# Four graph layers on one core: x turned by vector blocks and by DRAM instead of TensorE, short reciprocals, and products that fit either TensorE tile mode

## The chip, the cores and the metric

The kernel runs on one core of a Trainium2 chip. The metric is device time in microseconds (us), the median of several executions. Beside it stands one execution taken by the hardware profiler; all spans and durations come from that one. The engines are PE (TensorE, matrix products; PEld is its weight load), DVE (VectorE), ACT (ScalarE), POOL (GpSimd) and SP (SyncE, which only issues transfers). A record of PE is one pass: a float32 product makes two records, a transpose makes one.

## The reference

32 independent graphs of 512 nodes, each node with 256 features, go through four layers. Each layer ends in a residual sum and a layernorm. All of it is float32.

```python
# layer 0: h = (1+eps) x + adj @ x ;  x = LN(x + relu(h W1 + b1) W2 + b2)
# layer 1: graph attention, 4 heads: softmax over j of leaky_relu(e_dst_i + e_src_j) where adj > 0.5
#          x = LN(x + attention @ (x W) + bias)
# layer 2: 8 heads of 32: softmax over j of (q_i . k_j / sqrt(32) + log(adj + 1e-6))
#          x = LN(x + concat(heads) Wo.T + bo)
# layer 3: softmax over j of ((x W)_i . x_j * adj_ij), masked by nodemask ;  x = LN(x + attention @ x)
```

Products with x as the inner operand need x with features on the partitions (x transposed: 256 features in two tiles of 128 by 512 nodes). After each layernorm x has nodes on the partitions, so layers 1, 2 and 3 each begin by turning x.

## The kernel before, in words

`fast_path` first prepares the weights (`prepare`) and then handles the graphs one by one (`graph(g)`, 32 times). Nothing is emitted directly: each piece of work is a *step* of a `Plan`, with its engine, an assumed cost in us, the steps it comes after, and the buffers it takes and frees. `Plan.order` then walks through time with these costs and writes one order for all engines, a few graphs overlapping; which step goes first is set by a due time from the period and a long list of offsets by step name (the argument of `plan.run`). `Plan.run` emits the steps in that order. Each engine, and each DMA queue of SP and POOL, handles its instructions strictly in it; between engines there are semaphores. So a step that is late holds up everything behind it on its engine.

A PE step has a *mode*: the shape in which the 128x128 array is used. `""` is the whole array, `row` four tiles of 32 rows (layer 2's scores, L1203), `c32` four tiles of 32 columns (attention times values, L1043 and L1261; sums, L1081 and L1330), `r64` tiles of 64 rows and 32 columns (layer 2's sums, L1308). The planner adds the cost `CHANGE` of the new mode when it changes.

The steps around the change, by name and line, for one graph:

- `h`, `f`, `y` (L812, L835, L854): layer 0's three products, whole array. `residual_steps`, `norm_stats` and `norm_steps` (L681, L624, L641, L647, L655, L670) follow every layer: DVE adds to x and gathers statistics, POOL takes the power for rstd, DVE makes the shift, ACT scales x (`r`).
- `xt1`/`xe1`, layer 1's turn of x: 8 PE transposes into PSUM (L882) and two ACT copies. `v1` (L903): values.
- `features_first(2)` and `features_first(3)`, the turns of x for layers 2 and 3: 8 PE transposes (L1147) and two ACT copies (L1151) each. Then `q`, `k`, `v2` (L1166, L1184) for layer 2, and `i`, `t` (L1412, L1427) for layer 3; `p` (L1385) is layer 2's output product, `w` (L1456) is layer 3's attention times x.
- `normalise(o)`: layer 2's softmax denominators arrive in PSUM as [128, 512], where the 32 partitions of a head hold the same numbers. ACT copies them to SBUF (L1344), DVE takes the reciprocal of all 512 columns in two halves (`rc`, L1351), and multiplies y with it (`yd`, L1356).
- `la`: from the second graph on, adj is loaded in four transfers that read runs of 32 numbers (128 bytes), so that the 32x32 blocks lie turned round; four DVE transposes, which turn each 32x32 block in place, then finish the transpose (`at`, L778).
- `collect`, `fd`: POOL issues transfers that add layer 2's weights onto each other in SBUF, so that fewer sums are left to PE.

Of the kernel before, what the change touches and what calls it, by code (L numbers as in the profile page):

```python
# [9 lines left out]
F32 = mybir.dt.float32  # L10
# [38 lines left out]
class Plan:  # L49
# [12 lines left out]

    CHANGE = {"": 0.207, "row": 0.218, "c32": 0.143, "c64": 0.161, "r64": 0.166}
# [69 lines left out]
    def order(self, period, ahead, window, stay, rush=(), moves=(), edges=(0, (), 0, ())):  # L133
# [35 lines left out]
        while low < len(self.steps):  # L169
            found = []  # L170
            for (g, name), t in ready.items():
                s = self.steps[g][name]
                t = max(t, engine.get(s.eng, 0.0))
                change = self.CHANGE[s.mode] if s.eng == "pe" and s.mode != mode else 0.0
                for k, (kind, _, rest) in enumerate(s.take):
                    r, n = room[kind], sum(b[0] == kind for b in s.take[:k])
                    if len(r) <= rest + n:
                        break
                    t = max(t, r[n][0])
                else:  # L180
                    due = turn[g] * period - self.left[g][name] + shift(g, name) + stay * change
                    found.append((t, due, g, name, change))
            if not found:
                return math.inf, out
            first = min(found)[0] + near(low)
            _, t, g, name, change = min((due, t, *f) for t, due, *f in found if t <= first)
            s = self.steps[g][name]
            t += change
            if s.eng == "pe":
                mode = s.mode  # L190
            del ready[g, name]
            got = {}
            for kind, key, _ in s.take:
                got[key] = held[g][key] = (kind, room[kind].pop(0)[1])
            if s.eng:
                engine[s.eng] = t + s.us
            end = ends[g][name] = t + s.us
            last = max(last, end)
            out.append((g, name, t, got))
            for h, n in s.then:  # L200
                waits[h][n] -= 1
                if not waits[h][n] and h < opened:
                    ready[h, n] = self.ready(h, n, ends)
            for k in s.frees:
                fwaits[g][k] -= 1
                if not fwaits[g][k]:
                    key, after = self.frees[g][k]
                    kind, i = held[g].pop(key)
                    free = max(ends[g][a] + self.HOP.get(self.steps[g][a].eng, 0.0) for a in after)
                    room[kind].append((free, i))  # L210
                    room[kind].sort()
            todo[g] -= 1
            while low < len(self.steps) and not todo[low]:
                low += 1
                open_to(low + window)
        return last, out

    def run(self, tries):

        self.link()  # L220
        best = min((self.order(*t)[0], t) for t in tries)
        assert best[0] < math.inf
        for g, name, _, got in self.order(*best[1])[1]:
            self.slot[g].update((key, i) for key, (_, i) in got.items())
            self.steps[g][name].emit()
# [3 lines left out]
def fast_path(  # L229
# [103 lines left out]


# [249 lines left out]
    def graph(g):  # L584
        plan.graph()
        slot = plan.slot[-1]
        last = g == B - 1
        t = {"g": g}
# [101 lines left out]

        if g == 0:
# [73 lines left out]
        else:  # L765
# [16 lines left out]
            @step("atd", "dve", 0.6, row("at", NC))  # L782
            def _():
                full = t["AT"][:, 0, :]
                nc.vector.tensor_add(
                    t["ATd"],
                    bass.AP(full.tensor, full.offset, [list(full.ap[0]), [N + P, NC], [1, P]]),
                    selfw[:, None, :].to_broadcast([P, NC, P]),
                )
# [3 lines left out]
        for d in range(DC):  # L793

            @step(
                f"h{d}", "pe", 3.49,
                (("atd",) if g else row("ate", NC) + row("atd", NC)) + prev("h", d) + ("lx",),
                take=(f"p=h{d}",) + (() if d else ("C=hT",)),
            )
            def _(d=d):  # L800
                if d == 0:
                    t["hT"] = mid("hT", [P, DC, N], "hT")
                ph = t[f"ph{d}"] = bank(f"h{d}", [P, N], f"hT_ps_{d}")
                parts = []
                for m in range(NC):
                    parts.append((m, t["ATd"][:, m, :], blk(m)))
                    if m > 0:
                        parts.append((m, t["AT"][:, m, : m * P], slice(0, m * P)))
                    if m < NC - 1:
                        parts.append((m, t["AT"][:, m, (m + 1) * P :], slice((m + 1) * P, N)))  # L810
                for k, (m, moving, cols) in enumerate(parts):
                    nc.tensor.matmul(  # L812
                        ph[:, cols], t["x"][:, m, blk(d)], moving,
                        start=(k == 0), stop=(k == len(parts) - 1),
                    )
# [8 lines left out]
        for f in range(HC):  # L824
# [3 lines left out]
                take=(f"p=f{f}",) + (() if f else ("B=h1T/2",)),  # L828
            )
            def _(f=f):  # L830
# [3 lines left out]
                for d in range(DC):  # L834
                    nc.tensor.matmul(  # L835
                        ph, w1_sb[:, d, blk(f)], t["hT"][:, d, :], start=(d == 0), stop=(d == DC - 1)
                    )
# [9 lines left out]
        for c2 in range(NC // 2):  # L847

            @step(f"y{c2}", "pe", 3.45, row("fe", HC) + prev("y", c2) + ("^w2",), take=(f"p=y{c2}",))
            def _(c2=c2):  # L850
                py = t[f"py{c2}"] = bank(f"y{c2}", [P, 2, D], f"y0_ps_{c2}")
                for j in range(2):
                    for f in range(HC):
                        nc.tensor.matmul(  # L854
                            py[:, j, :], t["h1T"][:, f, blk(2 * c2 + j)], w2_sb[:, f, :],
                            start=(f == 0), stop=(f == HC - 1),
# [35 lines left out]
        for c in range(NC):  # L892
# [3 lines left out]
                take=(f"p=v1{c}",) + (() if c else ("C=v1",)),  # L896
            )
            def _(c=c):
# [3 lines left out]
                for d in range(DC):  # L902
                    nc.tensor.matmul(  # L903
                        pv, t["xT"][:, d, blk(c)], wg_sb[:, d, :], start=(d == 0), stop=(d == DC - 1)
                    )
# [247 lines left out]
        features_first(2, ("L2",))  # L1153
        bias_steps(3, row("xt2", DC))

        def proj(n, o):
            @step(
                f"{n}{o}", "pe", 1.72, row("xe2", DC) + prev(n, o) + (f"^we{n}",),
                take=(f"p={n}{o}",) + (() if o else (f"C={n}",)),
            )  # L1160
            def _():
# [3 lines left out]
                for d in range(DC):  # L1165
                    nc.tensor.matmul(  # L1166
                        pq, wT[n][:, d, blk(o)], t["xT2"][:, d, :], start=(d == 0), stop=(d == DC - 1)
                    )
# [5 lines left out]
        def values(c):  # L1174
            @step(
                f"v2{c}", "pe", 0.86, row("xe2", DC) + prev("v2", c) + ("^wev",),
                take=(f"p=v2{c}",) + (() if c else ("C=v2",)),
            )
            def _():
# [3 lines left out]
                for d in range(DC):  # L1183
                    nc.tensor.matmul(  # L1184
                        pv, t["xT2"][:, d, blk(c)], wT["v"][:, d, :], start=(d == 0), stop=(d == DC - 1)
                    )
# [153 lines left out]
        def normalise(o, after):  # L1340
            @step(f"nd{o}", "act", 0.49, (after,), take=(f"D=rdT{o}/1",), free=(f"d2{o}",))
            def _():
                t[f"rd{o}"] = strip(f"rdT{o}", [P, N], f"rdT_{o}")
                nc.scalar.copy(t[f"rd{o}"], t[f"d{o}"])  # L1344

            for i in range(2):
                half = slice(i * N // 2, (i + 1) * N // 2)

                @step(f"rc{o}{i}", "dve", 1.65, (f"nd{o}",))
                def _(half=half):  # L1350
                    nc.vector.reciprocal(t[f"rd{o}"][:, half], t[f"rd{o}"][:, half])  # L1351

                @step(f"yd{o}{i}", "dve", 0.34, (f"rc{o}{i}", f"no{o}"))
# [24 lines left out]
        for c2 in range(NC // 2):  # L1378

            @step(f"p{c2}", "pe", 1.73, (f"yd0{c2}", f"yd1{c2}") + prev("p", c2) + ("^weo",), take=(f"p=p{c2}",))  # L1380
            def _(c2=c2):
                py = t[f"py{c2}"] = bank(f"p{c2}", [P, 2, D], f"o2p_ps_{c2}")
                for j in range(2):
                    for d in range(DC):
                        nc.tensor.matmul(  # L1385
                            py[:, j, :], t["yT2"][:, d, blk(2 * c2 + j)], wT["o"][:, d, :],
                            start=(d == 0), stop=(d == DC - 1),
# [12 lines left out]
        features_first(3, ("L3",), src="x3")  # L1400
        for o in range(DC):
# [3 lines left out]
                take=(f"p=i{o}",) + (() if o else ("C=iT",)),  # L1405
            )
            def _(o=o):
# [3 lines left out]
                for d in range(DC):  # L1411
                    nc.tensor.matmul(  # L1412
                        pq, w3_sb[:, d, blk(o)], t["xT3"][:, d, :], start=(d == 0), stop=(d == DC - 1)
                    )
# [6 lines left out]
        for c in range(NC):  # L1421

            @step(f"t{c}", "pe", 1.72, row("ie", DC) + prev("t", c), take=(f"p=t{c}",))
            def _(c=c):
                pt = t[f"pt{c}"] = bank(f"t{c}", [P, N], f"s3_{c}")
                for d in range(DC):
                    nc.tensor.matmul(  # L1427
                        pt, t["xT3"][:, d, blk(c)], t["iT"][:, d, :],
                        start=(d == 0), stop=(d == DC - 1),
                    )  # L1430
# [19 lines left out]
        for c in range(NC):  # L1450

            @step(f"w{c}", "pe", 1.74, row("te", NC) + ("one",) + prev("w", c), take=(f"p=w{c}",))
            def _(c=c):
                py = t[f"py{c}"] = bank(f"w{c}", [P, D + 1], f"o3_ps_{c}")
                for m in range(NC):
                    nc.tensor.matmul(  # L1456
                        py, t[f"z3{m}"][:, blk(c)], t["x3"][:, m, :],
                        start=(m == 0), stop=(m == NC - 1),
                    )
# [538 lines left out]
```

## Time and profile before

| | before |
|---|---|
| median of 3 runs | 2814.2 us (2812.86 to 2814.27) |
| profiled execution, its own time | 2813.72 us |
| its span, first to last instruction | 2812.0 us |
| PE busy | 2777.1 us, 99% |
| DVE busy | 2235.4 us, 79% |
| ACT busy | 1774.5 us, 63% |
| software DMA queue (POOL's), share of 16 engines | 51.2% |
| hardware DMA queue (SP's) | 17.3% |
| granted TensorE clock | 0.997 |

A row of the cost groups reads: line, engine, operation, output and inputs by the program's names, shapes, count; then busy time in all and the mean of one in ns; then the idle time of the engine just before, and what ended it. A row of the timeline reads: start, length, engine, line, operation, names, shapes, count of instructions merged into the row, and in brackets the idle time before with what ended it. In the view by stretches a line gives the length, then for PE, PEld, DVE, ACT and POOL the busy time and the count, the clock and the DMA engines' share and rate. For PE the shape of the stationary tile comes first (128*32: 128 rows by 32 columns), then what streams through it. PE's records overlap, so its prices are read from start to start.

### The profile page before, as it was taken

What the parts mean: (1) busy time and instruction counts of PE and PEld (TensorE: products, weight loads), DVE (VectorE), ACT (ScalarE), POOL (GpSimd) and SP (SyncE); (2) the same over time, 40 slices, a digit from 0 to 9 for tenths busy, and PEclk for the clock granted to TensorE, in tenths of its full rate; (3) what the DMA queues carried; (4) which work ended last, traced back from release to release, by engine and by line L of the source; (5) the groups of instructions that cost most, each with busy time, mean ns of one, the idle gap of its engine ahead of it and who ended that gap; (6) DMA issues with size and microseconds to landing.
All of it is one profiled execution on the core that took longest, in us unless ns stands there. A gap on an engine that the chain in (4) does not pass through costs nothing.

```text
span 2812.0 us, 41564 instructions
## 1 busy us (share of the span) xinstructions
PE 2777.1 (99%) x15540; PEld 1549.1 (55%) x15540; DVE 2235.4 (79%) x4139; ACT 1774.5 (63%) x3438; POOL 450.9 (16%) x526
## 2 busy tenths in 40 slices
PE   8999999999999999999999999999999999999998
PEld 6544565555555555555555655555555555555544
DVE  3878779877779877788877788777798777887785
ACT  3767566676666675666665666766666756666564
POOL 1111111111111111111111111111111111111110
PEclk9999999999999999999999999999999999999999
DMA  8476777667787667786677776667776677667650
GB/s 172 90 160 123 154 143 155 134 137 145 145 158 145 131 139 146 139 171 134 137 141 148 143 160 133 135 143 149 153 144 135 139 146 143 136 134 137 135 104 16
DMA packets 350055, 388.74 MB, mean 138 GB/s; under 512 B 265036, under 2 KB 304920, under 8 KB 317976
## 3 DMA queue, kind: packets, MB, share of 16 engines
q0 software_dynamic: 45568, 277.89, 51.2%
q1 hardware_dynamic: 303296, 107.86, 17.3%
q8 instruction: 124, 2.03, 0.3%
q14 instruction: 83, 0.68, 0.1%
q10 hardware_dynamic: 984, 0.28, 0.0%
HBM read 141.38 MB, written 17.08 MB: 56 GB/s over the span
## 4 chain that ended last, share of the span: by engine, by line
PE 92%; DVE 3%; DMA 2%; ACT 2%; issue 1%; POOL 0%; ACTq 0%; SPq 0%; DVEq 0%; POOLq 0%
PE s L1203 9%; PE hT_ps L812 8%; PE o_ps L1261 8%; PE o_ps L1043 8%; PE h1T_ps L835 8%; PE s L1427 8%; PE o_ps L1456 7%; PE y_ps L854 7%; PE v_ps L903 4%; PE iT_ps L1412 4%; PE qT_ps L1166 4%; PE v_ps L1184 4%; PE o2p_ps L1385 4%; PE kT_ps L1166 4%; PE xT_t L1147 2%; DMA z<-z 1%
## 5 line engine op out<-in xcount | busy, mean ns | idle before, releaser
L1216 ACT ACTIVATE z<-s 128x512 f32<-128x512 f32 x1024 | 535.5, 605 | 214.4 <-PE s L1203 208.1
L1225 DVE SCALAR_TENSOR_TENSOR z<-AT,z 128x1024 f32<-128x1024 f32 x512 | 601.3, 1213 | 13.0 <-ACT z L1216 12.6
L1236 POOL DMA_DIRECT2D z<-z x186 | 164.1, 889 | 1686.2 <-DVE z L1225 522.8
L1351 DVE RECIPROCAL rdT<-rdT 128x256 f32<-128x256 f32 x128 | 214.3, 1721 | 229.2 <-ACT rdT L1344 229.2
L1010 ACT ACTIVATE z<-R_bc,nT,S 128x512 f32<-128x512 f32 x512 | 372.6, 814 | 3.3 <-DMA R_bc<-R_dram 3.2
L1021 DVE SCALAR_TENSOR_TENSOR z<-z,T,edge 128x512 f32<-128x512 f32 x512 | 347.4, 745 | 16.4 <-ACT z L1010 16.2
L670 ACT ACTIVATE x<-x,shift,rstd 128x256 f32<-128x256 f32 x508 | 264.0, 591 | 75.9 <-DVE shift L655 74.6
L1203 PE MATMUL s<-qT,kT 32*128 32x512 f32 x2048 | 288.9, 633 | 0.4 <-ACT kT L1172 0.4
L1261 PE MATMUL o_ps<-z,v 128*32 128x512 f32 x2048 | 264.2, 600 | 3.1 <-DVE z L1225 2.1
L1456 PE MATMUL o_ps<-x,z 128*128 128x257 f32 x1024 | 240.3, 386 | 3.2 <-ACT z L1216 2.5
L1071 DVE TENSOR_TENSOR z<-z 128x1024 f32<-128x1024 f32 (+1 forms) x256 | 237.0, 951 | 4.2 <-PE o_ps L1043 2.7
L1043 PE MATMUL o_ps<-z,v 128*32 128x512 f32 x2048 | 237.2, 599 | 0.0
L835 PE MATMUL h1T_ps<-hT,w_sb 128*128 128x512 f32 x512 | 234.3, 599 | 0.0
L1456 PEld LDWEIGHTS o_ps<-x,z 128*128 128x128 f32 x1024 | 189.2, 189 | 77.9 <-issue 46.3
L1427 PE MATMUL s<-iT,xT 128*128 128x512 f32 x512 | 229.3, 599 | 0.0
L854 PE MATMUL y_ps<-w_sb,h1T 128*128 128x256 f32 x1024 | 226.6, 379 | 0.0
L624 DVE BATCH_NORM_STATS2 st<-x 128x6 f32<-128x256 f32 x508 | 211.5, 416 | 9.3
L812 PE MATMUL hT_ps<-AT,x 128*128 128x384 f32 (+2 forms) x768 | 210.7, 384 | 0.5 <-ACT AT L761 0.5
L854 PEld LDWEIGHTS y_ps<-w_sb,h1T 128*128 128x128 f32 x1024 | 194.0, 190 | 27.4 <-ACT z L1216 0.8
L647 POOL TENSOR_TENSOR rstd<-ve,nhalf 128x4 f32<-128x4 f32 (+1 forms) x131 | 141.1, 1077 | 356.8 <-DVE ve L641 347.7
L841 ACT ACTIVATE h1T<-h1T_ps,b_sb 128x512 f32<-128x512 f32 x128 | 87.9, 687 | 147.7 <-PE h1T_ps L835 147.7
L1203 PEld LDWEIGHTS s<-qT,kT 32*128 32x128 f32 x2048 | 88.7, 183 | 160.8 <-issue 74.1
(162 smaller groups left out, 3763.2 us busy)
## 6 DMA issues: line engine op xcount, KB each, us to landing
z<-z POOLq DMA_DIRECT2D x186, 1024.0 KB, 8.2
x<-biases POOLq DMA_DIRECT2D x96, 512.0 KB, 9.6
R_bc<-R_dram SPq DMA_DIRECT2D x32, 1024.0 KB, 4.6
Ar<-in_adj_dram SPq DMA_DIRECT2D x124, 256.0 KB, 7.5
z<-z POOLq DMA_DIRECT2D x62, 512.0 KB, 7.0
x<-in_x_dram SPq DMA_DIRECT2D x32, 512.0 KB, 9.0
out_dram<-x SPq DMA_DIRECT2D x31, 512.0 KB, 4.1
xs_row<-xs_dram SPq DMA_DIRECT2D x32, 128.0 KB, 5.6
```

The lines of the kernel that those rows point to most:

```text
L812: nc.tensor.matmul(ph[:, cols], t["x"][:, m, blk(d)], moving, start=(k == 0), stop=(k == len(parts) - 1),)
L835: nc.tensor.matmul(ph, w1_sb[:, d, blk(f)], t["hT"][:, d, :], start=(d == 0), stop=(d == DC - 1))
L854: nc.tensor.matmul(py[:, j, :], t["h1T"][:, f, blk(2 * c2 + j)], w2_sb[:, f, :], start=(f == 0), stop=(f == HC - 1),)
L1010: nc.scalar.activation(t[f"e{h}"][:, c, :], t["Rbc"][:, h, :], AF.Relu, bias=t["nT"][:, h, c : c + 1], scale=t["S"][:, h, c : c + 1],)
L1021: nc.vector.scalar_tensor_tensor(z, z, t["T"][:, h, c : c + 1], t["edge"][:, c, :], op0=ALU.add, op1=ALU.mult)
L1043: nc.tensor.matmul(po[32 * q : 32 * q + 32, :], t["v"][:, c, hp * P + 32 * q : hp * P + 32 * q + 32], t[f"e{2*hp+q//2}"][:, c, :], start=( ...
L1203: nc.tensor.matmul(pk, t["k"][hs, o, blk(c)], t["q"][hs, o, :], start=True, stop=True)
L1216: nc.scalar.activation(t[f"E{k}"][:, j, :], t[f"ps{k}{j}"], AF.Exp, scale=QSCALE)
L1225: nc.vector.scalar_tensor_tensor(z, t["AT"][:, c, None, :].to_broadcast([P, 2, N]), ADJ_EPS, z, op0=ALU.add, op1=ALU.mult,)
L1261: nc.tensor.matmul(t[f"n{o}"][32 * j : 32 * j + 32, :], t["v2"][:, c, o * P + F2 * j : o * P + F2 * (j + 1)], t[f"E{k}"][:, j, :], start=( ...
L1427: nc.tensor.matmul(pt, t["xT3"][:, d, blk(c)], t["iT"][:, d, :], start=(d == 0), stop=(d == DC - 1),)
L1456: nc.tensor.matmul(py, t[f"z3{m}"][:, blk(c)], t["x3"][:, m, :], start=(m == 0), stop=(m == NC - 1),)
```

## The change

Five edits:

1. **Layer 2's x.** For all graphs but the first two and the last three (`near`), `moved` takes the place of `features_first(2)`. DVE transposes 32x32 blocks and writes them to another group of 32 partitions: for each output group b and each input group a, two instructions of 32 partitions by four blocks, 32 instructions in four steps (`xe2`). No PE step and no ACT copy is left, and no PSUM bank is taken.
2. **Layer 3's x.** For the same graphs `turned` takes the place of `features_first(3)`: SP stores x to DRAM (`xw3`), loads it back in four transfers of 128-byte runs (`xl3`), and DVE transposes the blocks in place (`xe3`, two instructions). It takes one more buffer of kind C (`xL3`).
3. **Reciprocals.** In `normalise` DVE transposes the denominators' blocks straight from PSUM (`nd`), takes the reciprocal of one column per block (`rc`, 16 numbers per partition), and transposes it back through a broadcast (`ne`). The ACT copy goes.
4. **Products in either mode.** All whole-array products of the graphs get mode `any`: the planner leaves PE in whole-array or `c32` mode if it is in one of them, and goes to `c32` otherwise; `product` emits a product whole or as four products of 32 output columns each. PE transposes keep the whole array.
5. **Order.** The argument of `plan.run` is replaced (the period, the offsets of all steps, the numbers of graphs with offsets of their own at the ends), so the order of every engine is new. `atd` also waits for `selfw`.

```diff
+    EITHER = {"": "", "c32": "c32"}
@@ Plan.order
-                change = self.CHANGE[s.mode] if s.eng == "pe" and s.mode != mode else 0.0
+                into = self.EITHER.get(mode, "c32") if s.mode == "any" else s.mode
+                change = self.CHANGE[into] if s.eng == "pe" and into != mode else 0.0
...
+    def product(out, lhsT, rhs, start, stop):
+        if plan.mode != "c32":
+            nc.tensor.matmul(out, lhsT, rhs, start=start, stop=stop)
+            return
+        for q in range(4):
+            part = slice(32 * q, 32 * q + 32)
+            nc.tensor.matmul(out[part], lhsT[:, part], rhs, start=start, stop=stop)
...
+        near = g < 2 or g >= B - 3
...
+        def turned(n, more, src):
+            @step(f"xw{n}i", "sp", 0.45, row(f"r{n}", NC))
+            def _():
+                t[f"xd{n}"] = dram.tile([N, D], F32, tag=f"x{n}_dram", name=f"x{n}_dram_{g}")
+                nc.sync.dma_start(t[f"xd{n}"].rearrange("(c p) d -> p c d", p=P), t[src][:, :, :D])
...
+            for a in range(4):
+                @step(f"xl{n}{a}i", "sp", 0.66, (f"xl{n}{a-1}i",) if a else (f"xw{n}",), ...)
+                def _(a=a):
...
+                    nc.sync.dma_start(
+                        t[f"xL{n}"][32 * a : 32 * a + 32].rearrange("j d (b i) -> j d b i", i=32),
+                        bass.AP(t[f"xd{n}"].tensor, t[f"xd{n}"].offset + 32 * a,
+                                [[D, 32], [P, DC], [32 * D, N // 32], [1, 32]]),
+                    )
...
+            for d in range(DC):
+                @step(f"xe{n}{d}", "dve", 0.66, row(f"xl{n}", 4) + prev(f"xe{n}", d), ...)
...
+                    nc.vector.transpose(t[f"xT{n}"][:, d, :], t[f"xL{n}"][:, d, :])
...
+        def moved(n, more, src, shared):
...
+            for b in range(4):
+                @step(f"xe{n}{b}", "dve", 1.3, row(f"r{n}", NC) + prev(f"xe{n}", b), ...)
+                def _(b=b):
...
+                    to = slice(32 * b, 32 * b + 32)
+                    for a in range(4):
+                        of = slice(32 * a, 32 * a + 32)
+                        out = t[f"xT{n}"][to].rearrange("j d (c a i) -> j d c a i", c=NC, a=4)[:, :, :, a, :]
+                        for d in range(DC):
+                            nc.vector.transpose(out[:, d], t[src][of, :, d * P + 32 * b : d * P + 32 * b + 32])
...
-        features_first(2, ("L2",))
-        bias_steps(3, row("xt2", DC))
+        if near:
+            features_first(2, ("L2",))
+            bias_steps(3, row("xt2", DC))
+        else:
+            moved(2, ("L2",), "x", False)
+            bias_steps(3, row("xe2", 4))
...
-            @step(f"nd{o}", "act", 0.49, (after,), take=(f"D=rdT{o}/1",), free=(f"d2{o}",))
+            @step(f"nd{o}", "dve", 0.62, (after,), take=(f"D=dT{o}/1",), free=(f"d2{o}",))
+            def _():
+                t[f"dT{o}"] = strip(f"dT{o}", [P, N], f"dT_{o}")
+                nc.vector.transpose(t[f"dT{o}"], t[f"d{o}"])
+            @step(f"rc{o}", "dve", 0.22, (f"nd{o}",))
+            def _():
+                few = t[f"rdc{o}"] = little([P, N // 32], f"rdc{o}")
+                nc.vector.reciprocal(few, t[f"dT{o}"].rearrange("p (b r) -> p b r", r=32)[:, :, 0])
...
+                nc.vector.transpose(t[f"rd{o}"], t[f"rdc{o}"][:, :, None].to_broadcast([P, N // 32, 32]))
-                @step(f"rc{o}{i}", "dve", 1.65, (f"nd{o}",))
-                    nc.vector.reciprocal(t[f"rd{o}"][:, half], t[f"rd{o}"][:, half])
...
-        features_first(3, ("L3",), src="x3")
+        if near:
+            features_first(3, ("L3",), src="x3")
+        else:
+            turned(3, ("L3",), "x3")
...
# h, f, y, v1, q, k, v2, p, i, t, w alike:
-                    nc.tensor.matmul(
-                        pq, w3_sb[:, d, blk(o)], t["xT3"][:, d, :], start=(d == 0), stop=(d == DC - 1)
-                    )
+                    product(pq, w3_sb[:, d, blk(o)], t["xT3"][:, d, :], d == 0, d == DC - 1)
...
-        plan.run([(86.8199, ...
+        plan.run([(82.399, ...
```

## The prediction

> **What bounds the kernel now.** I read the page first: span, busy shares, clock, then the chain that ended last.
>
> ```profile
> span 2812.0 us, 41564 instructions
> PE 2777.1 (99%) x15540; PEld 1549.1 (55%) x15540; DVE 2235.4 (79%) x4139; ACT 1774.5 (63%) x3438; POOL 450.9 (16%) x526
> PE 92%; DVE 3%; DMA 2%; ACT 2%; issue 1%; POOL 0%; ACTq 0%; SPq 0%; DVEq 0%; POOLq 0%
> ```
>
> PE works nearly the whole span and carries the chain. One steady period (the same order repeats for each middle graph) in the view by stretches:
>
> ```profile
> 1199.61:1284.87 85.26, 85.26 (x484) 47.93 (x482) 69.51 (x129) 55.02 (x108) 13.82 (x16) 1.00 0.71 144
> ```
>
> PE 85.26 of 85.26, DVE 69.5, ACT 55.0, the DMA engines 71%: nothing but PE's own work sets the period. The timeline of PE gives its prices by the distance from start to start:
>
> ```profile
> 1219.96 1.90 PE L1043 MATMUL o_ps<-z,v 128*32 128x512 f32 x16
> 1221.68 1.90 PE L1261 MATMUL o_ps<-z,v 128*32 128x512 f32 x16
> ...
> 1254.80 1.04 PE L1147 MATMUL xT_t<-ident,x 128*128 128x128 f32 x8
> 1255.77 1.06 PE L1261 MATMUL o_ps<-z,v 128*32 128x512 f32 x8
> 1256.76 3.70 PE L1166 MATMUL qT_ps<-xT,wqT 128*128 128x512 f32 x8
> 1260.30 1.88 PE L1166 MATMUL kT_ps<-xT,wkT 128*128 128x512 f32 x4
> 1262.02 0.60 PE L1147 MATMUL xT_t<-ident,x 128*128 128x128 f32 x4
> ```
>
> kT: 4 full-array records of 512 columns in 1.72 us, 0.43 each. o_ps in 128x32 tiles: 16 records in 1.72, so four tile records take the 0.43 of one full record: a product cut into four tiles costs PE the same. A transpose is 0.109. A run of one mode costs more than its records: o_ps x8 lasts 0.99 where two groups of four are 0.86. Taking every run so, in the steady stretch, a run costs beyond its records 0.201 us (full), 0.139 (128x32), 0.213 (32-row), 0.161 (64x32). This period has 21 runs, 3.9 us.
>
> [...]
>
> ```profile
> 1.07 0.47 DVE L507 MEMSET diag<- 32x32 f32 x4
> ...
> 1205.46 2.48 DVE L778 STREAM_TRANSPOSE AT<-Ar 128x512 f32<-128x512 f32 x4
> ```
>
> The answer for L507 gives each memset 85 ns, so 128 from start to start and 43 idle between; four whole-tile transposes (670, the last 704) take 2.48, so 593 from start to start and an overlap of 77.
>
> **The change, part by part (on PE).**
> 1. Transposes removed: layer 2's and 3's x for 27 of 32 graphs, 16 each: 27 x 16 x 0.109 = 47.1 us.
> 2. Products in either mode: their own time stays. The emitted orders have 248 full, 216 128x32, 223 row and 31 64x32 runs before, and 107, 203, 181, 31 after (14 for 21 in a steady period). 141 x 0.201 + 13 x 0.139 + 42 x 0.213 = 39.1 us.
> Together 86.2 us: with no new wait the span is 2725.8.
>
> **What it adds elsewhere.** ACT loses two copies of d and four of xT a graph, 0.59 each: 51.5. DVE loses four reciprocals:
>
> ```profile
> L1351 DVE RECIPROCAL rdT<-rdT 128x256 f32<-128x256 f32 x128 | 214.3, 1721 | 229.2 <-ACT rdT L1344 229.2
> L778 DVE STREAM_TRANSPOSE AT<-Ar 128x512 f32<-128x512 f32 x124 | 77.5, 680 | 2.5 <-DMA Ar<-in_adj_dram 2.3 <-issue 0.2
> ```
>
> 6.7 us a graph, and gains four 128x512 transposes (2.4), two reciprocals of 16 elements (0.6), two transposes for layer 3 (1.2) and, for layer 2, 32 block transposes of 32 partitions by 128 elements. With these at 0.24 (below) DVE comes to 69.5 - 6.7 + 4.2 + 7.7 = 74.7: no bound by itself. SP gains one 512 KB store and four 128 KB loads in runs of 128 bytes: 4,608 packets a graph, at q1's mean of 17.3% x 16 x 2812 / 303,296 = 26 ns, 7% more DMA share. The emitted order has some 43 us of PE work from layer 2's output products to iT; the way for x3 there (some 16 us of DVE order up to the shift, ACT 2.4, a store like out's 4.1, loads at or under Ar's 7.5 plus 2.6 of issuing, DVE 1.2) is some 34. Behind them on SP stands the next Ar, with most of a period in hand. I cost this at nothing; if the cover goes, each us late costs 27.
>
> **The step that decides: layer 2's blocks.** In the emitted order the PE work between the end of y (graph g+1) and kT (graph g) is iT 3.43, one o_ps 0.86, three score products 5.15, a run's change 0.14, eight transposes 0.87: 10.45 us. In the same stretch DVE does: add y, three statistics, ve, (POOL) rstd, shift, then 24 blocks, a statistic, ve, 8 blocks; kT waits for the last. The first part is in the trace of before, instruction for instruction:
>
> ```profile
> 1255.00 0.69 DVE L681 TENSOR_TENSOR x<-x,y_ps 128x512 f32<-128x512 f32 x1 [1.56 <-PE y_ps L854]
> ...
> 1257.46 0.17 DVE L641 TENSOR_SCALAR ve<-mv 128x4 f32<-128x4 f32 x1
> 1258.85 0.16 DVE L655 SCALAR_TENSOR_TENSOR shift<-mv,rstd 128x4 f32<-128x4 f32 x1 [1.22 <-POOL rstd L647]
> ```
>
> y's last slot ends at 1254.80, so the first block starts 4.13 after y. The statistic and ve inside take 0.77, the last end and the way to PE 0.28. Chain 5.18 + 32c against 10.45: kT waits 32c - 5.27, once a period, as y and kT are both PE's. It is nothing up to c = 0.165.
>
> No row shows c. [...] The input quadrant changes with every second block. [...] I take 0.24: a wait of 2.4 us, in some 25 periods (27 graphs, the first and last in another order): 60 us. Behind the waiting kT stand qT, a score product and layer 2's first scores, then ACT's exponents: all move with the period, so it isn't paid twice.
>
> Sum: 2812.0 - 86.2 + 60.3 = 2786.1. The profiled run was 2813.72, 1.7 above its span, and the median 0.5 above that: **2788 us**, 0.9% faster. The filling and draining losses of before (PE misses some 5% in the first 344 us) are taken as unchanged; that is worth +-10.
>
> **Rivals.**
> - *The blocks fit*[...]: the order leaves room for 0.165, and one operation's quadrants may cost nothing. The wait is 0 to 0.9 us, the time 2728 to 2751. Against it: the memsets.
> - *Every block waits for the last*[...]: the wait is 4.75 x 25 = 119 us, the time 2847, **slower**. It decides from c = 0.272, where the waits eat all 86. Against it: no semaphore stands between blocks in the emitted order, and each source quadrant serves two.
> - *PE cannot be fed in tiles*: a product in tiles has four times the instructions; hT then needs 160 in 3.49 us, 22 ns each. Before, 64 instructions (d_ps) pass at 13 ns each, but no stretch of 128 is denser than 35. At 30 ns two hT would take 2.6 us more a graph, and 70 us in all on top. A steady period of before shows no such limit, so it is small.
> - *The DRAM turn or the denominators' folds come late*: 1 us a period gives 27 us. DMA share 71% and slack of some 5 us speak against it.
>
> **How the numbers follow.** 2788 (own range 2765 to 2808) 0.46; blocks fit 0.32; every block waits 0.13; PE supply 0.05; late transfers 0.04. Eight in ten: 2722 (blocks fit, edges a little better) to 2830 (part of the slower case left out). One measurement tells 0.2% (5.6 us) from no change: faster 0.77, same 0.07, slower 0.16.
>
> **What would show it.** Steady period 84.5 us with one PE wait of 2 to 3 us at kT for DVE's transpose of x; blocks 0.24 apart, alternately close and far; hT, h1T and y in tiles as long as before; 14 runs a period; no wait at iT. Wrong if the period is 82.1 with no wait at kT, if that wait is over 3.5 us, or if tiled hT takes more than 3.5 us.

## The result and the profile after

The changed kernel takes 2845.4 us (median of four runs, 2839.9 to 2850.8) where the kernel before takes 2813.5 beside it: ratio 1.0115, 95% interval 1.0094 to 1.0137. It is 1.1% slower; 2788 and faster was predicted, in a range that ended at 2830. The profiled execution took 2846.3 us, its span is 2844.5, and TensorE's mean granted clock fell from 0.997 to 0.987.

The page of the changed kernel, its span, busy shares and the chain that ended last:

```profile
span 2844.5 us, 72934 instructions
PE 2717.2 (96%) x30624; PEld 1261.0 (44%) x30624; DVE 2372.0 (83%) x5121; ACT 1692.0 (59%) x3266; POOL 458.1 (16%) x526
PE 7%; DVE 1%; ACT 1%; DMA 1%; issue 0%; SPq 0%; POOL 0%; DVEq 0%; ACTq 0%
```

PE is busy 60 us less than before, and no longer through the span: 99% has become 96%. The chain could be followed for a tenth of the span only, so it says nothing here. Two neighbouring steady periods in the view by stretches (stretch, length, busy time and instructions of PE, its weight load, DVE, ACT and POOL, granted clock, share of the DMA engines, GB/s):

```profile
599.50:684.10 84.60, 82.11 (x1008) 37.55 (x1007) 75.53 (x165) 52.15 (x102) 14.22 (x16) 1.00 0.82 159
684.10:770.30 86.20, 83.70 (x1009) 38.27 (x1007) 75.63 (x165) 52.33 (x102) 14.24 (x16) 0.98 0.80 156
```

One period takes 84.6 us, as forecast; the next, of the same instructions, takes 1.6 longer at a clock of 0.98. Over 21 steady periods the mean is 85.64, from kT to kT (85.28 before). PE's timeline shows what differs. First the start of kT in the shorter period, then in the longer (start, length, the wait before it in brackets):

```profile
602.26 1.96 PE L340 MATMUL kT_ps<-xT,wkT 128*128 128x512 f32 x4 [2.49 <-DVE xT L783]
604.05 1.88 PE L340 MATMUL qT_ps<-xT,wqT 128*128 128x512 f32 x4
```

```profile
686.90 3.45 PE L340 MATMUL kT_ps<-xT,wkT 128*128 128x512 f32 x4 [2.50 <-DVE xT L783]
690.18 1.88 PE L340 MATMUL qT_ps<-xT,wqT 128*128 128x512 f32 x4
```

Both wait 2.5 us for DVE's blocks. After the second wait the same four records take 3.28 us from start to start instead of 1.79: PE runs at half clock (granted clock 0.50 in that stretch, cut out below) until qT. The view of PE's waits (us in total, times, longest) has this wait first, and others that the kernel before did not have:

```profile
PE kT_ps L340 <- DVE xT L783: 56.1, 24, 2.5
PE o_ps L344 <- DVE x L694: 11.7, 2, 9.3
...
PE o_ps L344 <- ACT z L1310: 4.9, 1, 4.9
...
PE iT_ps L344 <- DVE xT L741: 2.8, 1, 2.8
```

To put a number on each place I took, between successive PE records, the distance from start to start less the prices of the prediction (0.43 for a full record of 512 columns, a quarter of that in tiles, the extra of a run). What is left is lost time; it is good to some 4 us for a part of the run. Before, PE lost 33 us up to the first steady period, 1 in the steady part and 16 after it. Changed: 55, 79 and 35. The change therefore gave back its whole saving and 33 us more: 78 in the steady part, 22 at the start, 20 at the end.

### The profile page after: what moved, and what is told of

Its sections match the earlier page's. It is cut to its first block, busy times and chain, and to the rows that moved or that the text cites. A ratio compares the mean times of both kernels' runs of the same rounds, so it can differ in the third digit from the quotient of the medians.

```text
span 2844.5 us, 72934 instructions
## 1 busy us (share of the span) xinstructions
PE 2717.2 (96%) x30624; PEld 1261.0 (44%) x30624; DVE 2372.0 (83%) x5121; ACT 1692.0 (59%) x3266; POOL 458.1 (16%) x526
## 5 line engine op out<-in xcount | busy, mean ns | idle before, releaser
L683 ACT ACTIVATE x<-x,shift,rstd 128x256 f32<-128x256 f32 x508 | 278.0, 594 | 194.8 <-DVE shift L668 194.8
L1110 DVE SCALAR_TENSOR_TENSOR z<-z,T,edge 128x512 f32<-128x512 f32 x512 | 349.6, 744 | 21.6 <-ACT z L1099 21.5
L1297 PE MATMUL s<-qT,kT 32*128 32x512 f32 x2048 | 274.0, 625 | 0.0
L344 PE MATMUL o_ps<-x,z 128*32 128x257 f32 x3808 | 222.3, 384 | 18.3 <-DVE x L694 11.7
L783 DVE STREAM_TRANSPOSE xT<-x 32x128 f32<-32x128 f32 x864 | 214.2, 281 | 7.8 <-ACT x L683 1.6
L344 PE MATMUL y_ps<-w_sb,h1T 128*32 128x256 f32 x3456 | 197.1, 380 | 0.5 <-ACT h1T L933 0.5
L344 PEld LDWEIGHTS o_ps<-x,z 128*32 128x32 f32 x3808 | 123.2, 111 | 130.6 <-issue 33.5
L1543 DVE TENSOR_TENSOR z<-s,AT 128x512 f32<-128x512 f32 x128 | 85.4, 685 | 112.6 <-PE s L340 102.4
L344 PE MATMUL s<-iT,xT 128*32 128x512 f32 x1568 | 177.8, 592 | 0.0
L344 PE MATMUL hT_ps<-AT,x 128*32 128x128 f32 (+2 forms) x2448 | 172.5, 379 | 1.2 <-issue 1.2
L344 PEld LDWEIGHTS y_ps<-w_sb,h1T 128*32 128x32 f32 x3456 | 109.9, 110 | 100.4 <-ACT z L1310 16.7
```

Of the source, the lines that this page charges most:

```text
L344: nc.tensor.matmul(out[part], lhsT[:, part], rhs, start=start, stop=stop)
L683: nc.scalar.activation(t[into][:, c, :D] if into else xn, xn, AF.Identity, bias=t[f"shift{n}"][:, c : c + 1], scale=t[f"rstd{n}"][:, c : c ...
L783: nc.vector.transpose(out[:, d], t[src][of, :, d * P + 32 * b : d * P + 32 * b + 32])
L1110: nc.vector.scalar_tensor_tensor(z, z, t["T"][:, h, c : c + 1], t["edge"][:, c, :], op0=ALU.add, op1=ALU.mult)
L1297: nc.tensor.matmul(pk, t["k"][hs, o, blk(c)], t["q"][hs, o, :], start=True, stop=True)
```

## Experiments

Three theories at the outset. **A**: the wait for the 32 blocks is the steady loss, and the clock falls because PE waited. **B**: the clock falls because tiled products are denser work for PE, whatever it waits for. **C**: the loss lies at the ends and in feeding tiles. Numbers of graphs in the edits are those of the planner's lists, whose first is the preparation of the weights: 7 is the seventh graph. In the edit of e7 alone, g counts the graphs from 0. Except for e5, all edits are to the changed kernel, and the order that its planner gives is kept but for the moves named.

### e1, e4: larger blocks

```diff
-                        for d in range(DC):
-                            nc.vector.transpose(out[:, d], t[src][of, :, d * P + 32 * b : d * P + 32 * b + 32])
+                        nc.vector.transpose(
+                            out,
+                            t[src][of].rearrange("p c (d b j) -> p d c b j", d=DC, b=4)[:, :, :, b, :],
+                        )
```

e4 makes this edit for b < 2 alone.

> One edit, order kept: each block transpose of layer 2's x takes both column halves at once, 16 instructions of 32 partitions by 256 elements for 32 of 128. Theory A (the 32 blocks' chain makes the wait at kT, and TensorE's clock drops because of that wait): [...]16 take 5.9 to 6.5 us for 8.1, the wait at kT falls from 2.66 to between 0.4 and 1.0 us, 25 periods give 41 to 56 us, and most of the half-clock stretches (some 20 us) go too: 2770 to 2795 us, clock 0.993 or more. Theory B (the clock drops because of the dense tiled products, and the wait is apart from it): the wait falls as in A, the clock stays at 0.987: 2790 to 2805 us. Theory C (what was lost lies at both ends and in feeding tiles): 2835 to 2850 us.

> As the merged one, but only for the first two of the four groups of blocks: 8 instructions of 256 elements and 16 of 128. Theory A: the wait at kT is halfway, 1.6 to 1.9 us, the steady period 83.6 to 83.8 us without a clock drop; if the clock drop depends on the length of the wait there are fewer half-clock stretches than the one in two periods of the changed kernel, if it depends on there being a wait, as many. Theory B: as many as before. Time 2800 to 2825 us.

e1: 2817.0 us, ratio to before 1.0012 [1.0003, 1.0020]; e4: 2838.0, one run. The gain is real, 28 us, but short of every number given under A and B. The 5.9 to 6.5 us for 16 blocks were my estimate, which no trace showed. A block of 256 elements starts some 447 ns after the one before: each now comes from another quadrant (group of 32 partitions) than the last, and starts 14 ns after that one's end. So the 16 take 0.95 us less from the first to the last (8.06 for 9.01), not 2, and the wait falls by 0.77, to 1.89 us (2.18 in e4).

### e2: the same blocks, DVE's order changed

```diff
+        for g in range(6, 27):
+            put((g, "xe20"), (g + 1, "sh1.0"))
+            put((g - 3, "st42"), (g, "k0"))
+            put((g - 3, "va4.0"), (g, "k0"))
```

`put(what, ahead)` moves a step directly ahead of another in the emitted order. The reason is in the changed kernel's timeline of DVE:

```profile
1276.63 0.16 DVE L668 SCALAR_TENSOR_TENSOR shift<-mv,rstd 128x4 f32<-128x4 f32 x1 [1.22 <-POOL rstd L660]
1276.70 6.09 DVE L783 STREAM_TRANSPOSE xT<-x 32x128 f32<-32x128 f32 x24
1282.81 0.43 DVE L637 BATCH_NORM_STATS2 st<-x 128x6 f32<-128x256 f32 x1
...
1283.48 0.17 DVE L654 TENSOR_SCALAR ve<-mv 128x4 f32<-128x4 f32 x1
1283.68 2.04 DVE L783 STREAM_TRANSPOSE xT<-x 32x128 f32<-32x128 f32 x8
```

DVE idles 1.22 us for another graph's rstd in front of blocks that need nothing of it, and a statistic of a third graph stands ahead of the last eight.

> No instruction is changed, only DVE's order in graphs 6 to 26: the first 8 blocks go ahead of shift (they fill the 1.22 us in which DVE waits for POOL's rstd), and the statistic and ve of another graph (0.87 us) go behind the last 8 blocks. Theory A: the wait at kT falls from 2.66 to about 0.6 us in 21 periods, 44 us, and the half-clock stretches go with it: 2775 to 2795 us. Theory B (clock from the tiled products): 2795 to 2805 us at clock 0.987. Rival D (kT really waits for ACT's or a queue's work that ends just before the blocks): no gain, the wait is put down to another: 2835 to 2850 us.

2799.8 us, ratio 0.9950 [0.9933, 0.9966]: 0.5% faster than the kernel before, with the instructions of the changed kernel in another order. PE's timeline in a steady period:

```profile
760.07 1.95 PE L350 MATMUL kT_ps<-xT,wkT 128*128 128x512 f32 x4 [0.44 <-DVE xT L793]
```

The wait is 0.60 from start to start for 2.66, as worked out, and undisturbed periods take 82.58. The 45 us are slightly more than the 43 (21 periods) of the waits alone. Rival D falls. The time is 5 us above A's range. No wait at kT is followed by half clock any more (table below). What is left, besides the ends, are four periods in which PE loses 0.6 to 4 us at or just after layer 2's sums (d_ps); the longest of these waits, 1.6 us, is for a transfer with which POOL adds weights (z<-z). The prediction's rival of late folds thus shows, in small, once the period is shorter. It was not tested.

### e11: a longer wait

```diff
-                        for d in range(DC):
+                        for d in list(range(DC)) * (2 if b == 3 else 1):
```

> The changed kernel with the last 8 blocks of every graph made twice (the second writes the same values): the chain before kT is 2.0 us longer, the wait 4.7 us. Theory A1 (the length of the wait decides whether the clock halves after it): half-clock stretches in more than 14 of the 21 steady periods, most periods 86.7 plus 1.5 us. Theory A2 (the clock answers to something with its own rhythm): again in about every second. Time about 2900 us under both.

2923.8 us (one run), clock 0.970. The added blocks repeat quadrants, so they start 0.192 us apart and the wait is 4.21, not 4.7. After it PE runs slow in every period, at a granted clock of 0.96 over each of the two periods viewed, through kT and into qT (3.54 us from start to start for kT, 2.52 for qT):

```profile
786.37 3.75 PE L340 MATMUL kT_ps<-xT,wkT 128*128 128x512 f32 x4 [4.05 <-DVE xT L783]
789.91 2.68 PE L340 MATMUL qT_ps<-xT,wqT 128*128 128x512 f32 x4
```

A1 holds. Each trace also records the granted clock, and the half-clock stretches can be counted from it. Over 21 steady periods each:

| run | wait at kT, us | waits followed by half clock | us lost by it in kT and qT |
|---|---|---|---|
| e10 (below) | 0 | 0 | 0 |
| e2 | 0.60 | 0 | 0 |
| e1 | 1.89 | 5 | 8.5 |
| e4 | 2.18 | 10 | 17 |
| changed kernel | 2.66 | 11 | 17 |
| e11 | 4.21 | 21 | 49 |

Four more profiles with the wait of 2.66 (e3, e6, e7, e9) have 7, 7, 7 and 10. e2 has one half-clock stretch elsewhere, after the wait of d_ps named above. Theory B falls: e8 and e10 run the same tiled products without a half-clock stretch in the steady part (e10's granted clock is 1.00 in each of the three periods viewed), and e11 has one after each wait.

Which waits are followed can be read from the same record. In each of these traces all half-clock stretches begin on one grid, a step every 3.413 us, and last one or more whole steps, but for the last of a run, at its end (18 stretches in the changed kernel: sixteen of 3.41 us, one of 10.24, the last 9.62). Here the changed kernel's two waits from above, cut along its grid:

```profile
597.79:601.20 3.41, 1.98 (x20) 0.90 (x12) 3.24 (x14) 1.27 (x4) 0.88 (x1) 1.00 0.66 127
601.20:604.61 3.41, 2.35 (x6) 1.19 (x7) 3.03 (x9) 1.55 (x3) 1.05 (x2) 1.00 0.57 115
```

```profile
683.11:686.52 3.41, 1.29 (x12) 0.85 (x8) 3.24 (x14) 1.27 (x4) 1.48 (x2) 1.00 0.36 70
686.52:689.93 3.41, 3.03 (x4) 1.51 (x5) 2.39 (x6) 1.34 (x2) 0.44 (x1) 0.50 0.75 154
```

The first wait lies across a grid line: PE rests 1.43 us in one step and 1.06 in the next, and the clock stays. The second lies almost wholly in one step, PE rests 2.12 of 3.41 us in it, and the next step has half clock. In the steady part of the changed kernel each of the 11 half-clock stretches follows a step with 1.94 us of rest or more (2.41 at the most, so none of these steps was idle throughout), and no step with 1.88 or less is followed by one. In the other profiles the border lies between 1.6 and 2.0 us. So the waits of 0.60 us (e2) stayed below that border, those of 2.66 lay on either side of it by where they fell on the grid, and those of e11, 4.1 us of rest, leave 2.0 in one step wherever they fall.

### e5: tiled products alone, in the kernel before

The order before is kept; each square product is put in full mode or tiles by the cheapest run changes along it.

```diff
+                for m in ("", "c32") if s.mode == "any" else (s.mode,):
+                    cost, k = min((c + extra[m] * (m != k), k) for k, (c, _) in best.items())
+                    new[m] = (cost, (m, best[k][1]))
```

> The kernel before with one part of the change alone: its order of steps is kept, and each square product runs in full mode or in 128x32 tiles, whichever makes the run changes cheapest along that order (runs 718 -> 623: 248/216/223/31 -> 127/242/223/31). Theory A (a product costs the same in tiles, each run saved is worth 0.14 to 0.20 us, PE is the bound): 121 x 0.201 - 26 x 0.139 = 20.7 us less, 2792 us, steady period 84.5 us. Rival B (tiled products draw a lower clock or wait for their instructions): the saving is eaten, 2805 to 2820 us, clock under 0.995.

2805.8 us, ratio 0.9972 [0.9962, 0.9983]. The time lies in B's range, yet not for B's reason. A steady period went from 85.26 to 84.74, where three full runs fewer and one 128x32 run more are worth 0.46, and PE lost nothing there; the record shows half clock only near the start and the end (mean granted clock 0.995). So the price of a run holds, and B falls once more. Of the 20.7 us the start took back 8.6, with a wait of 5.2 us for ACT's copy of kT between 172 and 344 us, and the end 4.6. Why that copy came later was not tried.

### e3, e6, e9: what stood ahead of the late rows

The waits of 11.7 and 4.9 us lie between 362 and 390 us, where R_bc of layer 1 is late. SP's timeline in the changed kernel:

```profile
328.55 18.54 SPq L816 DMA_DIRECT2D Ar<-in_adj_dram  x4
347.19 3.13 SPq L1057 DMA_DIRECT2D xs_dram<-R_rows  x1
350.37 0.94 SPq L1040 DMA_DIRECT2D R_dram<-R_rows  x1
...
365.37 0.34 SPq L1047 DMA_DIRECT2D R_bc<-R_dram  x1
```

SP was held for 18.5 us by the issue of four adj loads in runs of 128 bytes, while the DMA engines were busy 90% or more in every slice of 1.5 us. The rows (R_rows) were ready on DVE at 340.5. In the kernel before, R_dram is issued at 339.3 and R_bc at 340.7.

> No instruction is changed, only SP's order once: the four loads of adj (and that of x) for the sixth graph go behind the loads of the third graph's layer-1 rows (R_bc, xs_row), in front of which they stood. Theory A (the stores of these rows stood 18.5 us behind the adj loads' issue on SP, and the loads went through a full DMA queue): the PE waits of 9.3, 4.9 and 2.4 us between 360 and 390 us go, 12 to 20 us gained: 2825 to 2833 us. Rival E (the DMA engines are full there anyway, and the work is only pushed on): under 4 us gained, PE waits for the sixth graph's adj or at the next turn of rows instead: 2840 to 2850 us.

> The changed kernel, SP's order moved once and now at the right place: the fifth graph's adj loads and its x go behind the third graph's R_bc load, so that the stores and loads of the third graph's rows no longer stand behind them on SP. Theory A: the PE waits of 2.4, 9.3 and 4.9 us between 362 and 390 us go, 12 to 20 us gained on the changed kernel's 2845: 2825 to 2833 us. Rival E (the DMA engines are full there in any case): under 5 us gained.

2849.1 and 2851.7 us, no gain. But neither says anything on the theory: I had taken the wrong graphs, and the same loads still stood ahead of the same rows. e9 moves the right ones:

```diff
+        for name in [f"la{a}{k}" for a in range(4) for k in ("i", ".q", "")]:
+            put((7, name), (5, "Rl.q"))
```

> The two moves on SP before this one were made at other places than the loads that stand ahead of the late rows: matching SP's transfers in the trace with the order one by one, the rows stored at 347 us are the fifth graph's, and the adj loads ahead of them the seventh's. Here, in the changed kernel, the seventh graph's four adj loads go behind the load of the fifth graph's R_bc. Theory A (the rows' stores wait on SP for these loads' issue): R_bc is issued some 10 to 18 us earlier, the PE waits of 2.4, 9.3 and 4.9 us at 362 to 390 us shrink to under 5 us together, 10 to 16 us less than the changed kernel: 2829 to 2838 us. Rival E (the DMA engines are full there in any case, or the work is only pushed on): under 4 us.

2833.8 us, ratio 1.0068 [1.0048, 1.0089], 11.5 us less than the changed kernel's median, as A said. SP's timeline and the one PE wait that is left there:

```profile
339.39 0.33 SPq L1048 DMA_DIRECT2D R_dram<-R_rows  x1
...
341.55 0.34 SPq L1055 DMA_DIRECT2D R_bc<-R_dram  x1
341.99 29.48 SPq L824 DMA_DIRECT2D Ar<-in_adj_dram  x4
```

```profile
368.25 1.95 PE L352 MATMUL o_ps<-x,z 128*32 128x257 f32 x32 [1.94 <-ACT z L1318]
```

In the profiled executions the loss at the start falls from 55 to 35 us, close to that of the kernel before (33), while the end loses 6 more. The start differs from execution to execution: eight other profiles without the move lose some 41 to 59 us there, e10 with it some 32. Rival E falls: the loads take as long as ever (29.5 us of issue), but nobody waits for them now.

### e7: layer 3's way through DRAM in the drain

In the drain the way is longer than in a steady period. Steady, then drain, from the store of x3 to the issue of its loads:

```profile
1246.97 0.37 SPq L709 DMA_DIRECT2D x_dram<-x  x1
...
1257.80 2.79 SPq L722 DMA_DIRECT2D xL<-x_dram  x4
```

```profile
2353.91 0.36 SPq L709 DMA_DIRECT2D x_dram<-x  x1
2354.46 0.44 SPq L1047 DMA_DIRECT2D R_bc<-R_dram  x1
2367.84 10.72 SPq L722 DMA_DIRECT2D xL<-x_dram  x4
```

DVE's transposes start at 1268.5 and 2386.0: 21.6 us and 32.1 us. In the drain the 1 MB load of R_bc is issued 0.55 us after the store, the loads' issue takes 10.7 us for 2.8, and DVE has to wait for them:

```profile
2386.00 1.30 DVE L741 STREAM_TRANSPOSE xT<-xL 128x512 f32<-128x512 f32 x2 [10.51 <-DMA xL<-x_dram]
```

```diff
-                nc.sync.dma_start(t[f"xd{n}"].rearrange("(c p) d -> p c d", p=P), t[src][:, :, :D])
+                if g < 26:
+                    nc.sync.dma_start(t[f"xd{n}"].rearrange("(c p) d -> p c d", p=P), t[src][:, :, :D])
```

The loads have the same condition, and the transposes of these graphs read x3.

> The changed kernel without layer 3's way through DRAM in graphs 26 to 28 alone (the store and the four loads are left out, and the two transposes read x3 itself: these graphs' layer 3 is not computed as the reference does). Theory A (in the drain the turn takes some 30 us instead of some 20, holds up DVE and a C buffer that the last graph's v waits for, and the clock halves after these waits): the waits of 2.8 us (iT) and 1.9 to 6.8 us (qT after ACT's v) go, with their half-clock stretches 8 to 17 us less: 2828 to 2837 us. Rival (other work ends as late there): under 4 us.

2839.7 us, ratio 1.0098 [1.0081, 1.0115]. The intervals of this and of the changed kernel overlap, so the time alone does not show a gain. By PE's records, the end loses 32.6 us, against 39.9 to 45.9 in nine other profiles of the changed kernel and its variants. But in the two remaining ones, e10 and the changed kernel's own, it loses 34 and 35 with layer 3's turn in place, because the wait of qT happened to be short or absent. In e7 that wait is gone, as A said, yet one profile cannot tell this from such a short case. So it is likely, not shown, that the turn costs 7 to 13 us at the end where qT waits long. The wait at iT stayed (3.5 us): it belongs to a graph before the 27th, and e7 does not test it.

### e8, e10: the edits together

e8 has e1, e2 and e6, e10 has e1, e2 and e9.

> The changed kernel with three of the edits together: blocks of both column halves at once, the first group of blocks ahead of shift and the foreign statistic behind the last, and SP's order at the third graph's rows. Theory A: no wait at kT in graphs 6 to 26, steady period 82.1 us, clock over 0.993, and the start's 12 to 20 us: 2767 to 2785 us. Theory B (clock falls by the tiled products themselves): period 82.1 where the clock is full but clock 0.988: 2785 to 2800 us.

> The run with merged blocks and DVE's order, 2777 us, with this move on SP in place of the earlier one. Theory A: another 8 to 16 us, 2761 to 2769 us. Rival E: 2773 to 2781 us.

e8: 2777.0 us, ratio 0.9868 [0.9846, 0.9890]. e10: 2762.2 us, ratio **0.9820 [0.9804, 0.9837]**: 50 us faster than the kernel before, and 83 faster than the change. A steady period of e10:

```profile
574.90:656.80 81.90, 81.90 (x1009) 37.68 (x1008) 74.56 (x149) 52.14 (x102) 14.23 (x16) 1.00 0.87 165
```

81.90 busy of 81.90 at full clock: no wait at kT. The 82.1 of the prediction without a new wait is reached, on the same products as the changed kernel. Two of the 21 periods lose 1.2 and 2.3 us at d_ps, as in e2.

### e12: hT in full mode

Between 900 and 1320 us and again from 1890 to 2220, in eight of 21 periods, PE stops 0.3 to 0.9 us inside hT in e10. The profile puts this down to "issue", time in which it shows nothing that PE waits for:

```profile
1272.26 0.85 PE L356 MATMUL hT_ps<-AT,x 128*32 128x384 f32 x8 [0.68 <-issue]
```

```diff
-                    product(ph[:, cols], t["x"][:, m, blk(d)], moving, k == 0, k == len(parts) - 1)
+                    nc.tensor.matmul(
+                        ph[:, cols], t["x"][:, m, blk(d)], moving, start=(k == 0), stop=(k == len(parts) - 1)
+                    )
```

> The fastest kernel so far (2762 us) with the two hT products of every graph always in full mode, order kept: 40 instructions for 160 each, and where they stood among tiles two more run changes a graph (0.34 us). Theory A (the 0.3 to 0.9 us that PE loses inside hT in about half of the steady periods is PE waiting for its instructions, and comes from the density of tiled products there): no such loss in any period, every undisturbed steady period 82.2 to 82.3 us. Theory B (the instructions arrive late at these places whatever is done): the loss stays or moves to the tiled product after or before hT, periods 82.5 to 83.1 us in the same places. Time 2755 to 2772 us under both.

A holds for hT: the period below took 82.56 us in e10, and the next one, 82.79 in e10, takes 82.30 here too.

```profile
1171.50:1253.80 82.30, 82.30 (x888) 38.17 (x887) 74.67 (x149) 52.15 (x102) 14.25 (x16) 1.00 0.87 163
```

The loss of 4.9 us in 21 periods is gone, for 0.39 us more in each: no gain. The edit changes the number of instructions and the mode at once, so that PE lacked instructions fits but is not told apart from a cost of the tiles themselves. The run took 2780.2 us, outside both forecasts, for another reason: DVE waited 17.0 us for adj at 344 us, and PE 13.3 for R behind it. These loads were issued from 304 us on, ahead of those that e9 moved. It is a single run; e10, with the same order on SP, has no such wait.

## Why the prediction was wrong

**What held.** The saving of 86.2 us: e10's undisturbed period is 81.9 for a forecast 85.26 - 3.19 = 82.07. The blocks' spacing c: 0.24 was taken, my estimate. Neither it nor the spacings that the two rivals assume stood in a trace of before; the one hint was the four memsets of L507, each on another group of 32 partitions, 43 ns apart. In the trace of the change the blocks are alternately 0.236 (overlapping the one before by 66 ns) and 0.273 (14 ns after its end), so 0.254 in the chain. "32c - 5.27" with it gives 2.86; measured 2.66, taken 2.4. The term of 60.3 us measured 58 (23 waits). The cover of the DRAM turn in the steady part: no wait there. The mechanism, its place and its size were right, and so was 84.5 us for a period that nothing else disturbs (84.64).

**The steps that failed.**
1. "Behind the waiting kT stand qT, a score product ... all move with the period, so it isn't paid twice." It is paid again, in the clock: 11 of 21 waits were followed by a stretch at half clock, 17 us in the steady part. No step priced what a PE at rest costs after the rest; until this change PE had not rested in the steady part, and the record of before has no half clock there (its three stretches begin at 215.3, 2683.2 and 2802.6 us).
2. "The filling and draining losses of before are taken as unchanged; that is worth +-10." They grew by 42 us: 22 at the start and 20 at the end. e9 shows that most of the 22 is SP's order, one set of adj loads issued ahead of another graph's rows: 20 us by the two profiles, 11.5 by the medians. The emitted order showed it beforehand; SP's queue in the fill was not read for the prediction. The cause of the 20 at the end stays open: in this profile the wait of qT was short, e7 loses only some 2 us less, and iT's wait (2.8 us, for the DRAM turn) and the rest were not separated.
3. "I cost this at nothing" of the DRAM turn: true of the steady part that was looked at, false in the drain, where DVE waits 10.5 us for the loads and PE 2.8 for DVE.
4. "PE cannot be fed in tiles" had 0.05 and some 70 us. It happens, in some eight of 21 periods and for 0.2 to 0.9 us: 3.8 us in all, and e12 shows that it comes with hT's tiles. The rival's size was far too large, and leaving it out of the sum cost little.

The sum again, from 2812.0: -86.2, +58 for kT, +17 for the clock, +4 for feeding, +42 for the ends, and some 3 less because the runs cost a little less than their prices: some 2844, where the span is 2844.5. Of the three theories, A names 75 of these 121 us and C 46.

**The rivals.** The one on the slower side named 2847 us by every block waiting (4.75 us at kT): nearly the right time for a wrong reason. "The blocks fit" was wrong on the price, though e2 shows that they nearly do once DVE's order is right.

## What to carry to other kernels

Price a new wait on PE at more than its length: here a wait of 2.7 us once a period cost 0.5 to 0.8 us more on average in half-clock work, and one of 4.2 us cost 2.3, while one of 0.6 us cost nothing more. Before a moved chain is called late by its own operations, look at what else stands in its queue: 2.1 of the 2.7 us were an idle wait and a foreign statistic that could stand elsewhere (e2), and one reordering of a loading queue was worth 11 to 15 us. Where an order is made anew, read the fill and the drain queue by queue; a saving shown in the steady part says nothing about them.

## What was not expected of the hardware

- Half clock (granted clock 0.50) came after waits of 1.9 to 2.7 us in a quarter to a half of the cases (5 to 11 of 21), after 4.2 us in all 21, and after 0.6 in none (table above). It began on a grid of 3.413 us, in the changed kernel after steps in which PE rested 1.94 us or more, in the other profiles from some 1.6 to 2.0 us.
- A VectorE block transpose of 32 partitions by 128 starts 0.192 us after one of the same quadrants (e11), 0.273 where the source quadrant changes, 14 ns after the end of the one before, and the one after a change 0.236 (both in the changed kernel). A change of quadrant thus cost 0.12 us over two instructions here. The slower successor, 0.236 for 0.192, was not expected.
- The issue of four loads of 256 KB in runs of 128 bytes held SP 18 to 30 us (18.5 in the changed kernel, with the DMA engines busy 90% or more in every slice of it, and 29.5 in e9), and everything behind them on SP with it.
- Among tiled products in a row (248 PE records in 14 us, with as many weight loads) PE stopped 0.2 to 0.9 us, in nearly the same graphs in the changed kernel and all its variants but e12. Why there and not in the other graphs stays open.
